# Four image layers in one kernel: first loads and evictions, the constants' products, a statistics product, layer 1's sums and the last evictions moved

## The chip, the cores and the metric

The kernel runs on one core of a Trainium2 chip. A core has five engines with a queue of instructions each: TensorE (PE) for matmuls and transposes, VectorE (DVE), ScalarE (ACT), GpSimd (POOL) and SyncE (SP), which here issues DMAs. PE writes to PSUM, which DVE and ACT empty into SBUF ("eviction"). An engine works through its queue in order, so an instruction that waits holds up what stands behind it. The metric is device time in microseconds (us), lower is better.

## The reference

The input `x` is float32 of shape (4, 64, 64, 64): four images of 4096 tokens with C = 64 channels. Four attention layers follow each other, each over the whole image:

```python
# layer 0: softmax(q k^T), read the other way round, gamma * out + x
attn = softmax(einsum('bic,bjc->bij', q, k)); out = einsum('bmn,bmc->bnc', attn, v); x = gamma * out + x
# layer 1: weights w / sigma_w (power step on w, u); phi and g max-pooled 2x2: 1024 keys
attn = softmax(theta @ phi.T); x = x + sigma * ((attn @ g) @ w_o + b_o)
# layer 2: group norm with 32 groups (per image row), attention per channel plane, residual
x = x + linear(attention(q, k, v of group_norm(x)))
# layer 3: group norm with 8 groups, attention scaled by 1/8, residual on the normalised h
h = group_norm(x); x = h + (softmax(q k^T / 8) v) wp + bp
```

## The kernel before

Tokens are kept transposed, two half images of 64 channels side by side on 128 partitions (`x_tile`, 128 x 2048). Wq and Wk of layers 0 and 3 are multiplied into one matrix beforehand ("form", `load_form` and `quadratic_form`); in layer 3 Wv and Wp likewise (`constants`).

A layer-0, layer-2 or layer-3 stage of one image is 64 *steps*. A step (`step`) issues two score tiles (`first`: four matmuls of 64 x 512 each, into an `s` tile), each followed by an exponential on ACT into a `p` tile, and then the sums of two earlier `p` tiles (`adds` or `then`) into accumulators. The 12 stages follow each other; their sums run a few steps behind their scores.

PSUM has eight banks: two `s` tiles of two banks each (pool `ps_s`), and four banks for accumulators (`ps_a`, `acc_tile`). Every score, projection, transposition and small product asks for the next `s` tile, and has to wait until the last tile in that buffer is read.

All other work is *background*: generators cut into pieces by `yield`. `background(tempo, ...)` sets how many pieces a step may take on average, and `advance` puts them at four places of a step: MID between its two groups of sums, LATE within the second, END after it. A piece marked ALONE goes to a MID and keeps LATE pieces (layer 1's scores) out of that step. `drain` runs what is left at a stage's end. So the order of the program is written by hand through these generators, and a `yield` more or less shifts all pieces behind it.

The places that matter here:

- *Opening.* ScalarE's queue loads Wq, Wk, bq of layer 0 and two of the eight first-half pieces of image 0 (L688 to L690, L651); SP loads the rest of the image (64 KB each) and then all other constants. PE transposes Wq and Wk (L715), multiplies them (L720, L721), transposes half the image (L892, in `transposed`), projects it to `q` (L859), transposes the other half, projects `q_swapped`, and only then starts layer 0's first step (L947). With `on="both"` the two halves of an eviction go to DVE and ACT, but from the same `s` tile.
- *Constants* (`constants`, L1523 on): small products with a MID between them: L1529, L1536 and L1538, L715, L720 and L721, L1551, L1556 and L1557, and for each of the four spectral norms L1582 and L1589.
- *Layer 1* (`layer1`): for image 0 with `bank=False`, sums added up on DVE; for images 1 to 3 with `bank=True`, sums in an accumulator (L1081). The denominators are L1097 on the running sums `zaccs` that DVE adds up (L1070), in an ALONE step, into an `s` tile.
- *Layer 3's statistics* (`before3`): DVE reduces the two halves (L1370), adds the two (L1372), and PE multiplies by the averaging matrix (L1374) in the same piece.
- *End.* The last block of queries: ACT copies one accumulator (L1210), DVE adds the other (L1211), PE multiplies by `wv3` (L1226) and sums the denominators (L1229, `lanes`), DVE takes the reciprocal (L1232), multiplies (L1234), adds `hb` (L1426), four DMAs write it (L1429). Then `rest_in_range` checks the softmax sums of this block (L1658 to L1665) and writes the flag `bad`. All engines load it (L1683) and branch over the second, general path (L1684).

## Time and profile before

| what | us |
|---|---|
| median of three timed runs | 3014.73 (3014.7 to 3015.45) |
| profiled execution | 3015.44 |
| its span, first to last instruction | 3013.7 |
| PE busy | 2979.1 (99%) |
| ACT busy | 1943.1 (64%) |
| DVE busy | 1769.4 (59%) |
| mean granted PE clock | 0.998 |
| from the span's start to the first score matmul (L947) | 15.4 |
| from the last sums to the span's end | 11.5 |

An engine's busy share says which engine bounds the whole, not which bounds a stretch. The chain of waits follows the last instruction back, at each step to what released it; in order of time its rows read "start, length, what". A row "PE s L947 x16" is one step's two score tiles (PE's records come in pairs, two for one float32 matmul). A row of waits reads "engine line <- who it waited for: total us, how often, the longest".

### The profile page before, as it was taken

The numbers are of one execution on the slowest core, as the hardware profiler recorded it, in microseconds if no ns is written. First come the engines' busy times: TensorE is split into PE (matmuls) and PEld (weight loads), VectorE is DVE, ScalarE is ACT, GpSimd is POOL, SyncE is SP. The second block draws the span as 40 slices with busy tenths as digits, with TensorE's granted clock in tenths as the row PEclk, the third lists the DMA queues.
The fourth block names the chain that finished last, engine by engine and source line by source line (L and its number), as shares of the span: only waits on it lengthen the run. The fifth ranks groups of instructions, "written<-read, shape, count | busy, mean of one in ns | idle before, by whom it ended". The sixth has DMA issues, their size and how long they took to land.

```text
span 3013.7 us, 64736 instructions
## 1 busy us (share of the span) xinstructions
PE 2979.1 (99%) x28501; PEld 1129.7 (37%) x28501; DVE 1769.4 (59%) x2058; ACT 1943.1 (64%) x2815; POOL 33.7 (1%) x35
## 2 busy tenths in 40 slices
PE   8999999999999999999999999999999999999998
PEld 3333233433444433344443333333343334333333
DVE  1221333588731068772017887777887777877777
ACT  6877777665578866557885655555555655555554
POOL 0000000000000000000000000000000000000000
PEclk9999999999999999999999999999999999999999
DMA  2010000000001000000000000000000000000000
GB/s 37 1 29 5 1 1 1 19 1 1 15 1 29 1 5 2 15 1 12 4 2 5 1 1 15 19 5 8 5 19 8 15 2 1 19 5 5 9 5 9
DMA packets 42081, 25.79 MB, mean 9 GB/s; under 512 B 39872, under 2 KB 39872, under 8 KB 40384
## 3 DMA queue, kind: packets, MB, share of 16 engines
q1 hardware_dynamic: 40464, 21.28, 3.4%
q8 instruction: 225, 3.69, 0.5%
q14 instruction: 64, 0.52, 0.1%
q10 hardware_dynamic: 1328, 0.30, 0.0%
HBM read 4.79 MB, written 4.19 MB: 3 GB/s over the span
## 4 chain that ended last, share of the span: by engine, by line
PE 97%; ACT 1%; DVE 1%; issue 0%; DMA 0%; ACTq 0%; DVEq 0%
PE acc L1203 29%; PE s L1168 29%; PE acc L972 15%; PE s L947 15%; PE s L1055 2%; PE acc L1081 1%; PE s L859 1%; ACT p L1061 1%; PE s L1081 1%; PE s L1226 1%; DVE zacc L1179 1%; PE s L878 1%; PE s L1312 0%; PE s L892 0%; PE s L1224 0%
## 5 line engine op out<-in xcount | busy, mean ns | idle before, releaser
L1173 ACT ACTIVATE p<-s 128x1024 f32<-128x1024 f32 x1024 | 994.7, 1022 | 710.8 <-PE s L1168 699.1
L1179 DVE TENSOR_TENSOR zacc<-zacc,p 128x1024 f32<-128x1024 f32 x960 | 1173.5, 1222 | 372.8 <-ACT p L1173 333.5
L951 ACT ACTIVATE p<-s 128x1024 f32<-128x1024 f32 x512 | 519.8, 1015 | 42.7 <-PE s L947 23.7
L1203 PE MATMUL acc<-p,v 64*64 64x512 f32 (+1 forms) x4456 | 526.5, 558 | 0.0
L972 PE MATMUL acc<-p,vs 64*64 64x512 f32 (+1 forms) x4224 | 514.0, 578 | 0.5 <-ACT vs L961 0.5
L1168 PE MATMUL s<-q,k 64*64 64x512 f32 x2048 | 495.0, 593 | 2.1 <-ACT p L1061 2.1
L1203 PE MATMUL acc<-p,hT 64*64 64x512 f32 x4096 | 494.1, 590 | 0.0
L947 PE MATMUL s<-xT,q 64*64 64x512 f32 x2048 | 488.3, 592 | 2.8 <-DVE v L879 0.6
L947 PE MATMUL s<-xT,q_swapped 64*64 64x512 f32 x2048 | 489.2, 592 | 0.0
L1168 PE MATMUL s<-q,xT 64*64 64x512 f32 x2048 | 486.8, 589 | 0.0
L1168 PE MATMUL s<-q,h_swapped 64*64 64x512 f32 x2048 | 479.3, 589 | 0.0
L1168 PE MATMUL s<-q,k_swapped 64*64 64x512 f32 x2048 | 476.9, 593 | 0.0
L953 DVE TENSOR_REDUCE all_z<-z 128x1 f32<-128x4 f32 x128 | 20.1, 157 | 622.3 <-ACT p L951 622.3
L1203 PEld LDWEIGHTS acc<-p,v 64*64 64x64 f32 x4456 | 179.8, 133 | 285.7 <-issue 280.6
L972 PEld LDWEIGHTS acc<-p,vs 64*64 64x64 f32 x4224 | 174.7, 133 | 266.4 <-issue 202.8
L961 ACT ACTIVATE vs<-v,all_r 64x64 f32<-64x64 f32 x512 | 176.6, 345 | 147.1 <-PE acc L972 72.3
L1203 PEld LDWEIGHTS acc<-p,hT 64*64 64x64 f32 x4096 | 156.3, 133 | 264.2 <-issue 263.4
L947 PEld LDWEIGHTS s<-xT,q_swapped 64*64 64x64 f32 x2048 | 146.3, 133 | 146.3 <-issue 111.4
L947 PEld LDWEIGHTS s<-xT,q 64*64 64x64 f32 x2048 | 146.4, 133 | 135.6 <-issue 109.1
L1168 PEld LDWEIGHTS s<-q,h_swapped 64*64 64x64 f32 x2048 | 143.9, 133 | 141.2 <-issue 136.2
L1168 PEld LDWEIGHTS s<-q,k 64*64 64x64 f32 x2048 | 140.5, 132 | 148.2 <-issue 99.3
L1168 PEld LDWEIGHTS s<-q,xT 64*64 64x64 f32 x2048 | 143.3, 133 | 140.2 <-issue 138.2
(205 smaller groups left out, 1564.8 us busy)
## 6 DMA issues: line engine op xcount, KB each, us to landing
k_swapped<-k SPq DMA_DIRECT2D x8, 512.0 KB, 6.1
h_swapped<-xT SPq DMA_DIRECT2D x8, 512.0 KB, 5.3
out_dram<-turned SPq DMA_DIRECT2D x62, 64.0 KB, 1.8
xin<-in_x_dram SPq DMA_DIRECT2D x24, 128.0 KB, 4.2
q_swapped<-q SPq DMA_DIRECT2D x6, 512.0 KB, 5.4
pg<-pg SPq DMA_DIRECT2D x8, 128.0 KB, 2.3
xin<-in_x_dram SPq DMA_DIRECT2D x14, 64.0 KB, 2.2
xin<-in_x_dram ACTq DMA_DIRECT2D x2, 64.0 KB, 2.8
```

What stands on the lines that cost most here:

```text
L859: nc.tensor.matmul(s[half(e), chunk(i)], w[half(i), half(e)], rhs[half(i), chunk(2 * j + (1 - e if exchanged else e))], start=True, stop=True,
L878: nc.tensor.matmul(s[:, ds(k * P, P)], rhs[:, ds((g * 8 + k) * P, P)], w, start=True, stop=True)
L947: nc.tensor.matmul(s[half(e), chunk(i)], queries(m, i, e), k[half(i), chunk(c)], start=True, stop=True)
L951: nc.scalar.activation(p, s, AF.Exp, accum_out=zs[m][:, c : c + 1])
L961: nc.scalar.activation(vs[half(e), :], v[half(e), m, :], AF.Copy, scale=rz[half(e), m : m + 1])
L972: nc.tensor.matmul(acc[c][half(i), cols], vs[half(e), :], ps[2 * t + n][half(e), chunk(i)][:, cols], start=(m == 0 and e == 0), stop=(m == ...
L1055: nc.tensor.matmul(ss[e][half(m), chunk(i)], pgs[0 if e == d else 1][r, ds(n * P + m * C, C)], th[r, chunk(2 * j + i)], start=True, stop=True,
L1081: nc.tensor.matmul(acc[quarter(q), :], g[:, k, :], ps[j, k][q // 2][:, chunk(q % 2)], start=(k == 0 or not bank), stop=(k == NK - 1 or not ...
L1168: nc.tensor.matmul(s[half(e), chunk(i)], k[(j + i) % 2][half(i), ds(j // 2 * P + e * C, C)], q[half(i), chunk(c)], start=True, stop=True,)
L1173: nc.scalar.activation(p, s, AF.Exp)
L1179: add = lambda: nc.vector.tensor_tensor(zaccs[c], p0, p, ALU.add)
L1203: nc.tensor.matmul(accs[c][e][half(i), cols], v[half(e), j, :], p[half(e), chunk(i)][:, cols], start=(j == 0), stop=(j == NB - 1),)
```

## The change

- *Opening.* Two loading queues for Wq and Wk; the four first-half pieces with r < 2 on SP, the others on ScalarE's queue; the bias and the second half behind them on SP. Matmuls on zeros (`keep_busy`) run between the form's operations. The first transposes and projections write two accumulator banks (`banks`, while `now[0] < 2`), one evicted by DVE, one by ACT. Both first projections come before the second half's transposes, which become the first background piece (`rest`).
- *Constants.* The transposition of Wv joins those of layer 2's weights, the form's products and the Wv-Wp product join the row sums' products in one `s` tile, and the four spectral norms run side by side: one piece with four L1582 products, one with four L1589 products, their columns handled 4 wide.
- *Statistics' product.* One `yield MID` between DVE's sum and PE's product in `before3`.
- *Layer 1's sums.* With `bank`, the denominators go to an accumulator bank, without the ALONE step in front.
- *End.* For the last image's last block `final` takes the place of `turn` and `last`: the denominators first, copies and sums in two halves of 256 columns, the range check on POOL (`rest_in_range`), and `bad` computed (`count_bad`) before the second half's multiply-add; DMAs alternate between SP and ScalarE's queue as before.

```diff
-    load = [nc.scalar.dma_start]
+    load = [nc.scalar.dma_start, nc.sync.dma_start]
...
+    def load_bias(n, bq):
+        load[0](form[n][1], bq.rearrange("(c o) -> c o", o=1))
...
         load[0](w[0:C, 0, :], wq)
-        load[0](w[0:C, 1, :], wk)
-        load[0](b, bq.rearrange("(c o) -> c o", o=1))
+        load[-1](w[0:C, 1, :], wk)
...
-    load_form(0, 0, a["L0_conv_Wq"], a["L0_conv_Wk"], a["L0_conv_bq"])
-    load[0] = nc.sync.dma_start
-    on_scalar = lambda r, i: nc.scalar.dma_start if i and r >= 2 else nc.sync.dma_start
-    load_x(state[0], [(slice(0, 8), on_scalar), (slice(8, 16), lambda r, i: nc.sync.dma_start)])
+    idle = scratch[:, 12 * P : 16 * P]
+    nc.vector.memset(idle, 0.0)
+
+    def keep_busy(n):
+
+        for _ in range(n):
+            nc.tensor.matmul(s_tile()[:, 0:256], idle[:, 0:P], idle[:, 0:256], start=True, stop=True)
+
+    load_form(0, 0, a["L0_conv_Wq"], a["L0_conv_Wk"])
+    load[:] = [nc.sync.dma_start]
+    load_x(state[0], [(slice(0, 8), lambda r, i: (nc.sync if r < 2 else nc.scalar).dma_start)])
+    load_bias(0, a["L0_conv_bq"])
+    load_x(state[0], [(slice(8, 16), lambda r, i: nc.sync.dma_start)])
...
+    def banks(on):
+
+        if on == "both" and now[0] < 2:
+            bank = [acc_tile(), acc_tile()]
+            return bank, bank
+        s = s_tile()
+        bank = [s[:, chunk(i)] for i in range(2)]
+        return bank if on == "both" else s, bank
+
...
-            evacuate("DVE", dst[:, 0:m], src[:, 0:m], bias)
-            evacuate("ACT", dst[:, m:], src[:, m:], bias)
+            evacuate("DVE", dst[:, 0:m], src[0], bias)
+            evacuate("ACT", dst[:, m:], src[1], bias)
...
-            z = s_tile()[:, 0:512]
+            z = acc_tile() if bank else s_tile()[:, 0:512]
...
         def finish(j):
-            yield ALONE
+
+            if not bank:
+                yield ALONE
...
         nc.vector.tensor_tensor(sums, stat[:, 0:1], stat[:, 1:2], ALU.add)
+        yield MID
         t = s_tile()[:, 0:1]
         nc.tensor.matmul(t, avg3, sums, start=True, stop=True)
...
+        def final(acc, sums):
+
+            z = acc_tile()[:, 0:8]
+            add_quarters(z, sums)
+            z_columns, r_columns = check_columns(8)
+            nc.vector.tensor_copy(z_columns, z)
+            nc.vector.reciprocal(r_columns, z_columns)
+            rest_in_range(z_columns, r_columns)
...
+            for m in range(2):
+                o, cols = o_tile("o")[:, 0:256], slice(m * 256, m * 256 + 256)
+                nc.scalar.copy(o, acc[0][:, cols])
+                nc.vector.tensor_tensor(o, o, acc[1][:, cols], ALU.add)
+                s = s_tile()[:, 0:256]
+                for n in range(2):
+                    nc.tensor.matmul(s[:, ds(n * P, P)], o[:, ds(n * P, P)], wv3, start=True, stop=True)
+                turned.append(s)
+            set_bad = count_bad()
+            for m, s in enumerate(turned):
...
+                if m == 0:
+                    set_bad()
...
-    st0 = transposed("both", s0)
-    next(st0)
-    alone(quadratic_form(0, 1.0))
-    next(st0)
-    queries0 = first_queries(s0)
-    next(queries0)
-    next(queries0)
-    alone(st0)
-    alone(queries0)
+    keep_busy(2)
+    form_transposes(0, s_tile())
+    keep_busy(1)
+    t = s_tile()[:, 0:P]
+    form_product(0, t)
+    form_scaled(0, 0, t, 1.0)
+    st0 = transposed("both", s0)
+    next(st0)
+    next(st0)
+    t = s_tile()[:, 0:1]
+    form_bias(0, t)
+    form_scaled(0, 1, t, 1.0)
+    keep_busy(1)
+    alone(first_queries(s0))
...
+        nc.tensor.transpose(s[0:C, 384:512], wvp[:, 0, :], ident)
...
+        yield MID
+        form_transposes(3, s_tile())
         yield MID
         t = s_tile()
...
+        form_product(3, t[:, 128:256])
+        form_bias(3, t[:, 513:514])
+        nc.tensor.matmul(t[:, 256:320], wvT, wvp[0:C, 1, :], start=True, stop=True)
+        nc.tensor.matmul(t[:, 320:384], bvb, wvp[0:C, 1, :], start=True, stop=True)
...
+        pt = s_tile()
+        for i, (r, d) in enumerate(shapes):
+            nc.tensor.matmul(pt[:, i : i + 1], ones[:r, :], sq[:r, i : i + 1], start=True, stop=True)
+        yield from inverse_norm(rn, pt[:, 0:4])
...
+        pt = s_tile()
+        for i, (n, dsts) in enumerate(spectra):
+            (r, d), (w, u, s, vb) = shapes[i], loaded[n]
+            nc.tensor.matmul(pt[:, ds(i * P, d)], vb[:r, :], w[:r, :], start=True, stop=True)
+        for i, (n, dsts) in enumerate(spectra):
+            d, (w, u, s, vb) = shapes[i][1], loaded[n]
+            nc.vector.tensor_copy(s, pt[:, ds(i * P, d)])
+            nc.vector.tensor_tensor(u, s, s, ALU.mult)
+            nc.vector.tensor_reduce(col(sq, i), u, AX.X, ALU.add)
...
-    background(1.0, second_half(s0), pause(6), constants(), loads(s1), pause(6), before0("DVE", s1), loads(s2))
+    background(1.0, rest(st0), second_half(s0, s0["v"]), pause(6), constants(), loads(s1), pause(6), before0("DVE", s1), loads(s2))
...
-    def rest_in_range():
+    def rest_in_range(z, r):
         assert checks[0] == NCHECK
...
+        nc.gpsimd.tensor_scalar(in_range[:, 0:count], z, SUM_MAX, None, ALU.is_le)
+        nc.gpsimd.tensor_scalar(in_range_r, r, 1.0 / SUM_MIN, None, ALU.is_le)
+        nc.gpsimd.tensor_tensor(in_range[:, 0:count], in_range[:, 0:count], in_range_r, ALU.mult)
+
+    def count_bad():
         nc.vector.tensor_reduce(least, in_range, AX.X, ALU.min)
-        t = s_tile()
+        t = acc_tile()
         nc.tensor.matmul(t[0:1, 0:1], least, ones[:, 0:1], start=True, stop=True)
-        nc.vector.tensor_scalar(bad, t[0:1, 0:1], -1.0, float(P), ALU.mult, ALU.add)
-
-    s3["after"] = rest_in_range
+        return lambda: nc.vector.tensor_scalar(bad, t[0:1, 0:1], -1.0, float(P), ALU.mult, ALU.add)
```

## The prediction

> **What bounds the kernel now.** The page first: who is busy, and who carries the chain that ended last.

> ```profile
> PE 2979.1 (99%) x28501; PEld 1129.7 (37%) x28501; DVE 1769.4 (59%) x2058; ACT 1943.1 (64%) x2815; POOL 33.7 (1%) x35
> ...
> PE 97%; ACT 1%; DVE 1%; issue 0%; DMA 0%; ACTq 0%; DVEq 0%
> ```

> TensorE (PE) is the bound almost everywhere, so an edit is worth only what it takes out of PE's own queue, or out of the two ends where PE does not yet, or no longer, run at full rate. The chain of waits was read next, in order of time, for the opening and for quiet and disturbed steps of the middle.

> ```profile
> 1.40 2.35 DMA scratch<-in_L_conv_Wk_dram
> 3.76 2.69 DMA xin<-in_x_dram
> 6.75 1.96 PE s L892 x8
> 8.73 0.70 DVE xT L838
> 9.48 2.60 PE s L859 x8
> 12.08 1.91 PE s L892 x8
> 15.38 2.57 PE s L947 x16
> ```

> The opening is serial, and PE is slow in it: eight transposes of L892 take 1.94 to 1.97 us here, and the same eight later take 1.02:

> ```profile
> 190.98 1.02 PE s L892 x8
> ...
> 104.82 0.86 PE acc L972 x8
> 105.68 0.31 PE s L1582 x2
> 105.99 1.02 PE acc L972 x8
> 107.01 1.72 PE s L947 x16
> ```

> The last four lines are the price of a small background piece: a plain step is 1.72 (scores) + 1.72 (sums); the piece adds its own 0.31 and 0.16 to the sums behind it (1.02 for 0.86), together 0.47. Next, who made PE wait, the layer-1 piece, and the one place where the clock fell:

> ```profile
> PE s L1374 <- DVE sums L1372: 4.1, 4, 1.2
> ...
> 656.44 0.99 PE s L1097 x8
> 657.43 1.02 PE acc L1203 x8
> ...
> 307.80:311.20 3.40, 3.40 (x20) 0.77 (x16) 2.08 (x2) 1.78 (x4) 0.00 (x0) 0.50 0.00 0
> ```

> The last of these (busy by engine, then granted clock, DMA share and GB/s) shows PE at half clock for 3.4 us in layer 1 of image 0. Last the end, from the instructions in order of time and from the line of the final branch:

> ```profile
> 3002.22 0.59 ACT L1210 COPY o<-acc 128x512 f32<-128x512 f32 x1 [4.03 <-PE acc L1203]
> 3006.15 0.69 DVE L1426 TENSOR_TENSOR turned<-turned,hb 128x512 f32<-128x512 f32 x1
> 3007.69 0.15 DVE L1665 TENSOR_SCALAR bad<-s 1x1 int32<-1x1 f32 x1 [0.37 <-PE s L1664]
> ...
> L1684 PEldq COMPARE_BRANCH  x1: 4035/4035/4035, 3008.6 to 3008.6; - x1
> L1684 ACTq EVENT_SEMAPHORE  x1: 17/17/17, 3011.8 to 3011.8; - x1
> ```

> The flag `bad` is the last thing computed; every engine then loads it (0.62 to 0.86), and PE's branch over the other path takes 4.04, while the output is long landing. ACT needs about 3.2 from its branch (3008.6) to its next event, DVE about as long. The span ends at 3013.7, some 0.9 after PE is through.

> **The change, part by part.** The working is against the profiled execution: 3015.44 us, of it 3013.7 span. The median of the three timed runs is 3014.73, so 0.7 is taken off at the end.

> 1. *Opening.* Before, the first exponential starts at 17.14. After: Wq and the four first-half loads of rows r>=2 are issued by ScalarE's queue, Wk and the other four by SP's; the bias load and the second half go behind them. ACT's issues cost 0.56 to 0.61, so its last one starts at 0.81+0.56+3x0.61 = 3.2 and lands 2.2 to 2.8 later (the issue table's medians): 5.4 to 6.0, where the chain had 6.45. Say PE begins the transposes at 5.9 (before 6.75). Each half then lies in two banks: DVE (0.69) and ACT (0.59) evict side by side instead of one after the other, and the second half's transposes leave the opening for the first main step. If PE is at full clock by then: transposes 1.02 with eviction behind until 7.6; both projections from 7.65 take 2x0.86 plus about 0.2 latency, to 9.6; DVE evicts the second by 10.35; scores of 1.07 (the L947 row); first exponential at 11.5. At half clock the transposes cost 1 more (12.5); if the projections are slow too, about 1.5 more (14.0). I take 11.7. What is late next: the second half's transposes, now in step 1, whose ACT eviction queues behind two exponentials (2 x 1.02), and values pushed one step on. Followed through the `s` buffers (each freed by one exponential or one 1.22 DVE eviction), the times from the first exponential are: step 2's scores 2.3, values 4.5, step 3 6.4, values 8.8, step 4 10.7, its second scores 12.1 (after DVE's `v`), step 5 14.8, step 6 19.5, and the first undisturbed step 23.0; before it is 40.34-17.14 = 23.2. So the gain is 17.14-11.7+0.2 = 5.6; bounds 3.1 and 6.5. SP carries one bias load more between the halves (0.6), covered, since the second half is wanted only at about 12.5 and the SP rows put its last issue near 8.5.
>    The four added matmuls on zeros cost nothing up to the input's landing; the last can delay the projections by half a microsecond, inside these bounds. [...]
> 2. *Constants.* The order of the changed program has 5 small PE pieces where there were 14. Before, the excess over a plain step of the 14 steps sums to 7.3: eight spectral pieces at 0.47 to 0.52, and six others at 0.40 to 0.75 (start to start of the steps). After: five transposes 0.79, the two form transposes 0.48, all products 1.7, the four L1582 products 0.31+3x0.24+0.16 = 1.2, the four L1589 1.3. But DVE now reads one `s` tile many times (seven reads of the products, 0.15 to 0.35 each, about 1.9; the fourth spectral copy as tenth instruction at 0.2, about 2.0), while the next-but-one scores want that buffer 0.86+0.16+0.86 = 1.9 later, and one batch also waits 0.4 for the row sums: stalls of 0.5 and 0.2. Gain 7.3-6.2 = 1.1; bounds -0.5 (both stalls 1 us longer) and 2.2 (none, and pipelined loads).
> 3. *Statistics' product.* DVE's sum of 0.15 then has a whole step to finish; PE's 4.1 of waiting goes. Behind it in PE's queue were sums and scores of the step, which is why all of it counts. The product still costs 0.47, as L1392's does (0.31 + 0.16). What follows slides by one or two steps in stages that have dozens to spare. Gain 4.1, bounds 3.5 and 4.2.
> 4. *Layer 1's sums.* For images 1 to 3, z takes a bank of the accumulators and needs no step of its own. Image 0's form is unchanged. Two L1097 pieces per image cost 0.99+0.16 = 1.15 each, some 1.2 by start to start. After, the first sits directly behind the L1081 sums, the second behind L1116. They keep 0.86 to 0.99, so each saves 0.2 to 0.3; six make 1.4, less a little for ACT's extra copy in a step of exponentials: 1.2. The new wait is z's on DVE's running sums, in front of scores: in the trace the last such add of image 1 ends at 639.13 (two L1070 rows from 636.78) and the sums before z at about 639.4, so it is just hidden. Bounds -1.5 (one 0.45 stall each) and 2.
> 5. *End.* z's product and reciprocal move ahead of the copies, the copy is halved, the range check goes to POOL, and `bad` comes between the last two multiply-adds. From 3002.2: z on DVE to 3003.24; two half adds (0.16+0.27 each, from the 512 and 1024 rows) to 3004.2; POOL's three small operations of 0.1 to 0.55 (its memsets and L748) to between 3003.7 and 3004.9; the rest of DVE to 3006.5 (3007.0 if POOL is slow), against 3006.84. `bad` is done near 3005.6, so PE's 0.65+4.04 run under the evictions, to 3010.4. Then ACT's queue is the last: two issues 0.9, load 0.62, branch to event 3.26: 3011.4, and 0.9 more gives 3012.3. Gain 1.4, bounds 0.3 (slow POOL, branches no faster) and 2.0; I take 1.3.
>    [...]

> Sum: 5.6+1.1+4.1+1.2+1.3 = 13.3. 3015.44-13.3 = 3002.1, and against the median 3001.4; I say 3001.5.

> **Rivals.**
> *Cold opening.* PE stays at half clock through the projections and the added matmuls only stand in the way. For it: the clock record starts at 14.2 and the matmuls before are slow though PE was busy from 9.5. Against: the zeros keep PE busy from about 1.5. Part 1 gives 3.1: 3004.
> *Better than summed.* The merged pieces hide, and the dip at 307.8 (its two rows 1.75 and 2.83 against 1.06 and 1.97 two steps on, 1.5 us) does not come back since the stage starts 7 us earlier. All upper bounds would be 3015.44-17-1.5; a plausible share is 17 in all: 2997.7.
> *The covers are gone.* z waits for DVE in all six places (1.2, one add, each) and both merged batches stall 1 us longer: 13.3-7.2-1.6 = 4.5: 3010, within 0.2%.
> *Slower.* The dip recurs. Layer 1 of image 0 has some 15 steps of 6.68 in which PE stops for an exponential (1.03); only one falls to half clock in this trace. The stage starts at another time, and if the fall came in every step it would cost 15 x 1.5 = 22: 3023. From nine falls on, it eats the 13.3. Against: the other fourteen steps do not trigger it.
> *It does not do what it says.* The program's order shows all the moves, so only the clock remains open, which is the first rival.

> **How the numbers follow.** Forecast 0.63, cold opening 0.16, better 0.12, covers gone 0.07, slower 0.02. The forecast's own range, from parts 2, 4 and 5 half-way to their bounds, is 2998.5 to 3005. The range to hold 8 in 10 reaches into the cold opening with weak parts 2 and 4, and into the better case: 2996.5 to 3007. About 0.2%, 6 us, is what a measurement of this kernel tells from nothing, so 3008.7 is the border: faster 0.91, same 0.06, slower 0.03.

> **What would show it.** Part 1: first exponential near 11.7, second-half transposes after it in about 1.02, a plain step by 35. Part 2: five pieces, the last before 100 us, with 0.2 to 0.6 of waiting on DVE behind the products and the second batch. Part 3: no wait of L1374's line on the sums. Part 4: z's wait on DVE under 0.2. Part 5: `bad` before the last two DVE operations, PE's branch ended before ACT's, under 10.5 us from the last sums to the end. Wrong it would be by a slow clock at the first projections, or several falls near 300 us.

## The result, and the profile after

The changed kernel takes 3005.69 us (median of 8 runs, 3004.41 to 3006.02) where the kernel before takes 3014.75 (8 runs beside it, 3013.88 to 3015.49). The ratio is 0.9969, with a 95% interval of 0.9958 to 0.9980. The time lies in the range that was given, and the direction is right, but the sum was too large: 13.3 us were forecast, and between the two profiled executions (3015.44 and 3005.78) there are 9.7.

The page of the changed kernel, busy time by engine and then the chain that ended last by engine:

```profile
PE 2979.2 (99%) x28509; PEld 1133.0 (38%) x28509; DVE 1760.1 (59%) x2003; ACT 1943.8 (65%) x2816; POOL 34.1 (1%) x32
...
PE 98%; ACT 1%; SPq 0%; DVE 0%; issue 0%; DMA 0%; ACTq 0%; DVEq 0%
```

PE's busy time is the same 2979 us, but it is not the same work: the matmuls on zeros add 4.5 us at the start (2.07, 1.22 and 1.22), and about as much went elsewhere. DVE's 1% of the chain is gone. Where the time went is read by setting the start of the same exponential in both traces side by side (there are 1664, and the program has them in the same order):

| stage, up to the exponential number | before | after | gain so far | gain of the stage |
|---|---|---|---|---|
| opening, 13 | 41.27 | 40.02 | 1.24 | 1.24 |
| constants and image 1's preparation, 107 | 218.30 | 215.62 | 2.69 | 1.45 |
| first pieces of layer 1 of image 0, 161 | 317.95 | 313.89 | 4.05 | 1.36 |
| layer 1 of images 1 to 3, 971 | 1745.54 | 1741.26 | 4.28 | 0.23 |
| the four statistics, 1481 | 2676.67 | 2668.20 | 8.47 | 4.19 |
| the end, span | 3013.71 | 3003.70 | 10.01 | 1.54 |

Differences are formed before rounding. 0.35 of the 10.01 is lost outside the span, which makes 9.66. The table says at once where the forecast was off: the opening gave 1.2 instead of 5.6, layer 1's sums 0.2 instead of 1.2, and 1.4 came from a place that the sum did not count.

The opening of the changed kernel: PE's instructions in order of time (weight loads left out), then ACT's.

```profile
5.97 1.97 PE L916 MATMUL acc<-ident,xin 128*128 128x128 f32 x8 [0.18 <-DMA scratch<-in_L_conv_bq_dram]
...
7.87 0.58 PE L736 MATMUL s<-scratch 64*128 64x1 f32 x2
...
8.39 1.22 PE L703 MATMUL s<-scratch 128*128 128x256 f32 x2
...
9.54 3.47 PE L883 MATMUL acc<-xT,A 64*64 64x512 f32 x16
...
12.83 1.02 PE L971 MATMUL s<-xT,q 64*64 64x512 f32 x4
```

```profile
7.98 0.59 ACT L870 COPY xT<-acc 128x512 f32<-128x512 f32 x1 [2.90 <-PE acc L916]
11.64 0.69 ACT L872 ACTIVATE q<-acc,Ab 128x512 f32<-128x512 f32 x1 [3.08 <-PE acc L883]
13.11 0.69 ACT L872 ACTIVATE q_swapped<-acc,Ab 128x512 f32<-128x512 f32 x1 [0.78 <-PE acc L883]
14.98 1.02 ACT L975 ACTIVATE p<-s 128x1024 f32<-128x1024 f32 x1 [1.18 <-PE s L971]
```

The eight transposes (L916) take 1.97, as slowly as before. ACT has emptied its half at 8.57, but the projections (L883) start at 9.54: a matmul on zeros (L703) stands in front of them. And they take 3.47, not 1.9. By these times PE is at half clock until 12.65, where the trace's record of the granted clock begins: the transposes before it start 0.213 apart, the same transposes of the second half, at 15.72, 0.109 apart. So the first exponential is at 14.98.

The other parts, from the chain in order of time: the two batches of spectral products, and the statistics' product L1409 (L1374 before) beside its twin L1427 (L1392).

```profile
89.48 1.06 PE s L1668 x8
...
101.00 1.14 PE s L1678 x8
```

```profile
1764.91 0.31 PE s L1409 x2
...
1779.14 0.31 PE s L1427 x2
```

L1409 has disappeared from the list of PE's waits; its steps take 3.91 to 3.94, like L1427's. Layer 1's denominators (L1121, L1097 before), first and second of image 1, same view:

```profile
634.56 1.00 PE acc L1105 x8
635.55 0.86 PE acc L1121 x8
```

```profile
692.67 0.86 PE s L1140 x8
693.53 1.00 PE acc L1121 x8
694.53 1.02 PE acc L1234 x8
```

And the end, in order of time (DVE and ACT), then the line of the branch:

```profile
2993.75 0.65 ACT L1480 COPY o<-acc 128x256 f32<-128x256 f32 x2 [4.03 <-PE acc L1234]
...
2996.71 0.14 DVE L1761 TENSOR_SCALAR bad<-acc 1x1 int32<-1x1 f32 x1
2996.78 0.40 DVE L1490 TENSOR_TENSOR turned<-s,all_r 128x256 f32<-128x256 f32 x1
2997.21 0.43 DVE L1494 TENSOR_TENSOR turned<-turned,hb 128x256 f32<-128x256 f32 x1
```

```profile
L1779 PEldq COMPARE_BRANCH  x1: 4152/4152/4152, 2997.5 to 2997.5; - x1
...
L1779 PEldq EVENT_SEMAPHORE  x1: 51/51/51, 3001.7 to 3001.7; - x1
L1779 ACTq EVENT_SEMAPHORE  x1: 17/17/17, 3002.2 to 3002.2; - x1
```

`bad` is now written ahead of the last two operations of DVE. PE loads it under them, its branch of 4.15 starts at 2997.49, just before the last of them ends (2997.64), and is through before ACT's queue. From the last copy to the span's end there are 9.95 us instead of 11.49.

### The profile page after: what moved, and what is told of

Read it like the earlier page. It is cut to its first block, busy times and chain, and to the rows that moved or that the text cites. A ratio compares the mean times of both kernels' runs of the same rounds, so it can differ in the third digit from the quotient of the medians.

```text
span 3003.7 us, 64700 instructions
## 1 busy us (share of the span) xinstructions
PE 2979.2 (99%) x28509; PEld 1133.0 (38%) x28509; DVE 1760.1 (59%) x2003; ACT 1943.8 (65%) x2816; POOL 34.1 (1%) x32
## 3 DMA queue, kind: packets, MB, share of 16 engines
HBM read 4.79 MB, written 4.19 MB: 3 GB/s over the span
## 4 chain that ended last, share of the span: by engine, by line
PE 98%; ACT 1%; SPq 0%; DVE 0%; issue 0%; DMA 0%; ACTq 0%; DVEq 0%
PE acc L1234 30%; PE s L1199 30%; PE acc L996 15%; PE s L971 14%; PE s L1079 2%; PE acc L1105 1%; ACT p L1085 1%; PE s L883 1%; PE s L1105 1%; PE s L1262 1%; PE s L1346 0%; PE s L902 0%; PE s L1260 0%; PE s L1443 0%; PE s L1366 0%; PE s L1051 0%
## 5 line engine op out<-in xcount | busy, mean ns | idle before, releaser
L1210 DVE TENSOR_TENSOR zacc<-zacc,p 128x1024 f32<-128x1024 f32 x960 | 1174.1, 1223 | 372.2 <-ACT p L1204 334.4
```

What stands on the lines that cost most here:

```text
L1210: add = lambda: nc.vector.tensor_tensor(zaccs[c], p0, p, ALU.add)
```

## The experiments

Two theories were to be told apart for the opening, both of them assumptions of the author's. The first: the clock rises after a stretch of some 3.4 us that PE fills with work (the fall in the trace of before lasts 3.413, from 307.793 to 311.206), such stretches lie at another place in each execution, and the kernel's short pauses waste them. The second: the clock rises at a fixed time, and the matmuls on zeros only stand in the way. For the other parts the question was whether each gives what the table of stages says. Every kernel is the changed one with one edit, except its repetition and the last kernel, which has two. The line numbers of an experiment can be some lines off. Clock and first exponential are from its one profiled execution:

| kernel | median us (runs) | profiled | clock rises at | first exponential | clock falls in layer 1, image 0 |
|---|---|---|---|---|---|
| before | 3014.75 (8) | 3015.44 | 14.25 | 17.14 | 307.79 |
| changed | 3005.69 (8) | 3005.78 | 12.65 | 14.98 | no |
| changed, again | 3005.47 (7) | 3005.88 | 14.48 | 15.38 | no |
| opening of before | 3007.37 (10) | 3007.22 | 15.86 | 18.01 | no |
| no zeros | 3004.51 (6) | 3004.56 | 10.65 | 13.60 | no |
| no last zeros | 3004.43 (6) | 3004.97 | 11.68 | 14.04 | no |
| zeros fill the pauses | 3004.77 (6) | 3003.94 | 7.99 | 12.85 | no |
| short fillers | 3005.17 (6) | 3005.61 | 10.89 | 13.98 | 304.44 |
| 10 us of zeros | 3007.33 (9) | 3007.33 | 7.02 | 16.62 | no |
| constants of before | 3007.06 (9) | 3008.94 | 13.03 | 15.16 | 306.58 |
| statistics of before | 3009.72 (11) | 3010.01 | 12.94 | 15.21 | no |
| sums of before | 3005.88 (7) | 3005.97 | 14.31 | 15.38 | no |
| end of before | 3007.26 (10) | 3007.32 | 12.50 | 14.89 | no |
| sums ahead of scores | 3003.18 (5) | 3002.34 | 12.95 | 14.35 | no |

The kernel before, run beside each of the four groups of experiments that follow, had medians of 3013.89, 3014.80, 3014.41 and 3014.88 us; so medians of different groups can be compared to about 1 us. The traces compare more closely: from the first to the 13th exponential all twelve traces with the changed order of the first steps take 25.03 to 25.05 us, and the two with the order of before 24.12 and 24.13. So what differs between openings is the first exponential, and 0.9 that the changed order gives back.

**The opening of before**

```diff
-    load = [nc.scalar.dma_start, nc.sync.dma_start]
+    load = [nc.scalar.dma_start]
...
-        if on == "both" and now[0] < 2:
+        if False:
...
-    keep_busy(2)
-    form_transposes(0, s_tile())
-    keep_busy(1)
...
+    st0 = transposed("both", s0)
+    next(st0)
+    form_transposes(0, s_tile())
...
-    background(1.0, rest(st0), second_half(s0, s0["v"]), pause(6), ...
+    background(1.0, second_half(s0, s0["v"]), pause(6), ...
```

> The changed kernel with the opening of before: its load order, no zero matmuls, first evictions from one score tile, the second half's transposes ahead of the first step. Theory: the opening is worth only 1.2 us of the 9.1, because the first exponential moved 2.2 and the transposes moved into the steps give 0.9 of it back; expected first exponential at 17.1, first step without background work again 1.2 us later than in the changed kernel, median 3006.9 (3006.5 to 3007.4). Rival: the forecast's 5.6 holds and another part lost the time; then 3011.

Median 3007.37, 1.7 to 1.9 above the changed kernel, as the first theory had it; the span is 1.54 longer. But its first exponential is not at 17.14, as was expected: the same opening is 0.9 later here. 0.1 of that is there from the transposes on (6.88 for 6.75), the rest comes in matmuls that run at half clock for longer (the second projection takes 1.97 instead of 1.23), since the clock rose at 15.86 instead of 14.25. So the same opening had a clock that rose at different times, and one trace of it is worth no more than about 1 us. The changed opening scatters less: six traces have it (the changed kernel's two, and those of the kernels with constants, statistics, sums and end of before), the clock rises at 12.50 to 14.48, and the first exponential is at 14.89 to 15.38. This run undoes the opening as a whole; what its load order, its two banks and its moved transposes give each was not run.

**No zeros, and no last zeros**

```diff
-    keep_busy(2)
     form_transposes(0, s_tile())
-    keep_busy(1)
     t = s_tile()[:, 0:P]
...
-    keep_busy(1)
     alone(first_queries(s0))
```

> The changed kernel without any of its four matmuls on zeros. The product for the bias then ends near 8.4 and the projections can start when ACT has evicted, at 8.65 instead of 9.54. Theory (the clock rises after a stretch of about 3.4 us of PE work without a pause): PE's work before 8.65 has pauses, so the clock rises only near 12 to 15; projections 3.4 us at half clock, first exponential 14.0 to 15.0, total within 1 us of the changed kernel. Rival (the clock rises at a fixed time, 12.65, whatever PE does): first exponential at 13.6 to 13.9, total 1.0 us less, 3004.6.

The second kernel takes away the last `keep_busy(1)` alone:

> The changed kernel without the last of the zero matmuls, the one in front of the projections (8.39 to 9.54 in the trace). Theory: projections start at 8.65, but PE then pauses 0.2 in front of them; if such a pause costs a whole stretch, the clock rises at 14 or later and the first exponential is at 14.4 to 14.8; if it does not, it rises near 12.65 as before and the first exponential is at 13.8. Rival (the zero matmul costs nothing because the projections waited for something else): first exponential unchanged at 14.98. Total 3004.5 to 3005.7.

Without the last zeros, PE's instructions in order of time:

```profile
7.92 0.58 PE L736 MATMUL s<-scratch 64*128 64x1 f32 x2
...
8.43 3.65 PE L883 MATMUL acc<-xT,A 64*64 64x512 f32 x16
```

The projections start 1.1 earlier and the first exponential 0.94 earlier (14.04); the last kernel of the table has this opening too, and there it is at 14.35. So the rival that the zeros cost nothing is gone. Without any zeros the clock even rose at 10.65 and the first exponential was at 13.60. Both kernels are 1.0 to 1.3 faster by their medians, little more than what groups can be compared to, but in the direction that the traces show. Neither theory had forecast this: the first one had the clock rise between 12 and 15 without zeros, and 13.60 and 3004.51 are the numbers of the second (13.6 to 13.9, 3004.6). Its cause, a fixed time of 12.65, is excluded all the same, by the rises of these two and by the changed kernel's own repetition, where the clock rose at 14.48:

> The changed kernel once more, beside the others, for a second record of its clock. Theory (windows of 3.41 us that lie at another place in each execution; the first one that PE fills without a pause raises the clock): PE has no pause from 5.97, so the clock rises between 9.4 and 12.8, at another time than 12.65; the first exponential moves with it, between about 13.6 and 15.0. Rival (a fixed time): 12.65 and 14.98 again. Median 3005.0 to 3006.0.

The theory missed here too. It had a rise by 12.8, because PE is busy without a pause from 5.98. The clock rose only at 14.48. So a window that PE fills by the trace's busy time was not enough here.

**Filling the pauses**

```diff
-    def keep_busy(n):
+    def keep_busy(*widths):
 
-        for _ in range(n):
-            nc.tensor.matmul(s_tile()[:, 0:256], idle[:, 0:P], idle[:, 0:256], start=True, stop=True)
+        for n in widths:
+            nc.tensor.matmul(s_tile()[:, 0:n], idle[:, 0:P], idle[:, 0:n], start=True, stop=True)
...
-    keep_busy(2)
+    keep_busy(256, 256, 128)
...
-    keep_busy(1)
+    keep_busy(256, 64)
...
-    keep_busy(1)
+    keep_busy(64)
```

> The zero matmuls sized to fill PE's pauses at 3.2, 4.7 and 8.5 (widths 256, 256, 128 ahead of the form's transposes, 256 and 64 ahead of the product, 64 ahead of the projections; pauses left under 0.2). Theory: PE works without a pause from 1.5, the clock rises by 8.4 at the latest, the projections from 8.7 take 1.9, the first exponential starts at 11.8 to 12.2, 3 us earlier than in the changed kernel; total 3002.5 to 3003.5. Rival (fixed time of the clock, 12.65): first exponential at 13.7 to 14.0, total 3004.6.

The clock rose at 7.99 and the projections ran at full speed. PE in order of time:

```profile
6.48 1.81 PE L916 MATMUL acc<-ident,xin 128*128 128x128 f32 x8
...
8.89 2.01 PE L883 MATMUL acc<-xT,A 64*64 64x512 f32 x16
```

2.01 stand against 3.47. The first exponential came at 12.85, 2.1 earlier than in the changed kernel, not 3: the wider zeros pushed the form back (its transposes by 0.4, the input's by 0.5). The median of six runs is only 0.7 to 0.9 lower, which two groups do not tell apart, and nearer to the rival's 3004.6 than to the theory's 3002.5 to 3003.5. Three runs lie at 3003.48 to 3003.94, the traced one among them, and three at 3005.59 to 3006.47; when the clock rose in these is not known. The second try kept the fillers small:

```diff
-    keep_busy(2)
+    keep_busy(256, 256, 32)
     form_transposes(0, s_tile())
-    keep_busy(1)
+    keep_busy(256, 32)
...
     form_scaled(0, 0, t, 1.0)
+    keep_busy(64)
...
-    keep_busy(1)
     alone(first_queries(s0))
```

> The changed kernel with zero matmuls that bridge the short pauses (32 columns ahead of the form's transposes and ahead of the product, 64 behind the product until the input lands) and none ahead of the projections. Theory: PE is without a pause from 1.5, the clock rises between 4.9 and 8.4 wherever the windows lie, the projections start near 8.45 at the full clock; first exponential at 12.4, or down to 11.5 if it rises before the transposes. Total 2.6 us under the changed kernel's profiled 3005.78, 3003.2, where no fall of the clock in layer 1 of image 0 adds some 1.5. Rival (the 32-column fillers are too short to count): the clock rises between 9.4 and 12.9 as in the changed kernel, first exponential 13.5 to 14.2.

This theory failed: the clock rose at 10.89, as the rival said. PE in order of time:

```profile
4.13 1.49 PE L703 MATMUL s<-scratch 128*128 128x256 f32 x4
5.54 0.79 PE L732 MATMUL s<-scratch 64*128 64x128 f32 x2
6.27 0.69 PE L703 MATMUL s<-scratch 128*128 128x64 f32 x2
6.75 1.91 PE L916 MATMUL acc<-ident,xin 128*128 128x128 f32 x8
```

No row has idle time in front of it: by the trace PE is busy without a pause from 1.50, as the theory wanted, and the clock stayed low all the same. So it is not idle time in the profile that held the clock down here. The fillers also moved the product from 5.00 to 5.54 and the input's transposes from 5.97 to 6.75. The last test puts dense work ahead of everything:

```diff
-    keep_busy(2)
+    keep_busy(*[512] * 6)
...
-    keep_busy(1)
     t = s_tile()[:, 0:P]
...
-    keep_busy(1)
     alone(first_queries(s0))
```

> The changed kernel with six matmuls on zeros of 512 columns ahead of everything else and no others: PE is dense from 1.5 to about 11, and the form and the input wait behind them. Theory (the first window of 3.41 us that PE fills raises the clock, zeros or not): it rises between 4.9 and 8.4, and the matmuls on zeros are shorter behind that point; total 1 to 3 us more than the changed kernel. Rivals: zeros do not count, then it rises 3.4 to 6.8 us after the last of them, near 15 to 19; a fixed time, then near 12 to 15.

The line of the zeros in that kernel, durations as minimum, median and maximum in ns, and PE in order of time:

```profile
L703 PE MATMUL s<-scratch x12: 592/888/1222, 1.5 to 9.1; 128*128 128x512 f32 x12
```

```profile
1.50 8.14 PE L703 MATMUL s<-scratch 128*128 128x512 f32 x12 [1.50 <-DVE scratch L698]
...
10.99 1.06 PE L916 MATMUL acc<-ident,xin 128*128 128x128 f32 x8
```

The clock rose at 7.02, in the middle of the zeros, which then ran in 0.59 instead of 1.06, and the transposes behind took 1.06. So zeros counted as work, and 5.5 us of wide matmuls on them (1.50 to 7.02) were enough in this execution.

What has to fill a window is read here from the same traces, afterwards, and was not tested. Count only the columns that PE streams, at the speed that the transposes show at half clock (0.213 us per 128 of them, from start to start in the changed kernel). Then the windows after which the clock rose were filled to between 0.78 and 1.00, and those after which it did not to at most 0.81. In the changed kernel two windows were missed: one filled to 0.72 (six gaps of 0.13 to 0.23 between the columns, nearly all of it inside what the profile counts as busy) and one filled to 0.70 (the bias product L736 and the zeros around it). With the short fillers the missed window from 4.07 to 7.48 has 0.68. The border is near 0.8 in these traces; windows of 0.78, 0.79 and 0.81 did nothing, others of 0.78 and 0.81 were enough, so this count alone does not decide it. The transposes have to be counted: they are 1.46 of the 3.41 us in the window of 0.78 that was enough (4.58 to 7.99, where the zeros fill the pauses).

**One part undone at a time.** The statistics' product:

```diff
         nc.vector.tensor_tensor(sums, stat[:, 0:1], stat[:, 1:2], ALU.add)
-        yield MID
         t = s_tile()[:, 0:1]
```

> The changed kernel without the new piece boundary between DVE's sum and PE's product of the statistics. Theory: the four steps of the product return from 3.94 to 5.2, 4.8, 4.8 and 5.1, and PE's wait for the sums to 4.1; median 4.2 more than the changed kernel, 3009.9. Rival (the wait had gone because the whole schedule shifted): under 2 more.

PE's waits in it:

```profile
PE s L1408 <- DVE sums L1406: 4.1, 4, 1.2
```

Median 4.0 to 4.3 more. The constants one by one again (`constants` as it was, with a piece for each product; its first lines):

```diff
         for i in range(4):
             nc.tensor.transpose(wt[:, i, :], wl2[:, i, :, :].rearrange("p j f -> p (j f)"), ident[:C, :C])
-        nc.tensor.transpose(s[0:C, 384:512], wvp[:, 0, :], ident)
...
-        form_product(3, t[:, 128:256])
-        form_bias(3, t[:, 513:514])
...
+        form_transposes(3, s_tile())
+        yield MID
+        t = s_tile()
+        form_product(3, t[:, 0:P])
```

> The changed kernel with the constants' products of before, one by one. Theory: fourteen small pieces cost 7.3 over plain steps where the five merged ones cost 5.9; median 1.4 more than the changed kernel, 3007.1. Rival (the merged pieces' stalls on DVE eat the gain): within 0.3.

Median 1.4 to 1.6 more, and 1.44 between the exponentials 1 and 109 of the two traces. The five merged pieces have 5.9 us over plain steps, the fourteen small ones 7.3. The sums of layer 1:

```diff
-            z = acc_tile() if bank else s_tile()[:, 0:512]
+            z = s_tile()[:, 0:512]
...
-            if not bank:
-                yield ALONE
+            yield ALONE
```

> The changed kernel with layer 1's denominators as before: an own step in front and a score tile for all images. Theory: the bank saves only some 0.1 an image (0.3 where the product now stands directly behind sums of the same tile shape, nothing behind the output product, and 0.2 lost when DVE's work slides into the steps of the evictions); median within 0.5 of the changed kernel, 3005.5 to 3006.1. Rival (the forecast's 1.2 holds and is lost elsewhere): 3006.8.

Median 0.2 to 0.4 more, with a first exponential that was 0.40 later; between exponentials 287 and 971, that is layer 1 of all three images, the difference is 0.23. The chain of this kernel, at the place of the first denominators:

```profile
652.79 0.99 PE s L1121 x8
653.78 1.02 PE acc L1233 x8
```

0.99 and 0.16 behind it (1.02 for 0.86) is what the product costs alone. In the changed kernel the first one costs 0.86, with sums of the same tile shape in front of it (`128*32` both), and the second one 1.00 and again 0.16, behind a product of `64*64`. The end:

```diff
-            st, wv3, "p (i n) f -> p n i f", last, not_before, "done3", final if st["b"] == B - 1 else None
+            st, wv3, "p (i n) f -> p n i f", last, not_before, "done3"
...
+            if c == NC - 1 and "after" in st:
+                st["after"]()
...
+    s3["after"] = rest_in_range
```

> The changed kernel with the end of before: copies and sums in one piece, the range check behind the last eviction. Theory: from the last sums to the span's end 11.5 instead of 10.0, median 1.5 more, 3007.1. Rival (the engines' branches set the end wherever the flag is computed): under 0.5 more.

Median 1.6 to 1.8 more; from ACT's last copy to the span's end 11.41 instead of 9.95.

**The falls of the clock, and a faster kernel.** In three of the fourteen profiled executions the clock fell for one window in layer 1 of image 0. Busy time by engine, then granted clock, in the windows around the fall with the short fillers:

```profile
301.03:304.44 3.41, 2.88 (x36) 0.78 (x32) 0.93 (x3) 2.20 (x4) 0.00 (x0) 1.00 0.00 0
304.44:307.85 3.41, 3.41 (x24) 0.84 (x20) 1.75 (x2) 2.05 (x5) 0.00 (x0) 0.50 0.00 0
```

and the same in the changed kernel, where it did not fall:

```profile
302.76:306.18 3.42, 2.89 (x34) 0.66 (x34) 1.51 (x4) 2.13 (x3) 0.00 (x0) 1.00 0.00 0
306.18:309.59 3.41, 3.41 (x42) 1.21 (x38) 1.02 (x1) 3.22 (x7) 0.00 (x0) 1.00 0.00 0
```

Both windows hold PE's 0.53 of pure waiting for an exponential behind the second piece's scores (L1079, 1.6 us in that piece). What differs is where in the window the wait ends: at 2.82, 3.16 and 3.31 of 3.41 in the three falls, at 0.63 to 2.70 in the changed kernel and the nine other traces that have this wait. The place alone is not enough: ten other waits of 0.53 in this layer end between 2.82 and 3.31 of their window too (the first piece's in the changed kernel at 2.89), and no fall followed. The two steps that a fall touches take 15.07 to 15.33 instead of 13.89, so 1.2 to 1.4 us. Why the clock fell at this wait is open: by the count of columns the windows ahead of the falls are filled to 0.71 to 0.73, but so are many that no fall followed.

The wait itself is PE's longest (8.0 us in 15 steps), so the last run took it away, together with the last matmul on zeros:

```diff
+            order = [(m, e) for m in range(2) for e in range(2)]
+            for m, e in order if bank else sorted(order, key=lambda me: me[1]):
...
                 yield LATE
+                if n and not bank:
+                    add(*todo[n - 1])
                 accumulate = scores(*todo[n])
-            if n:
+            if n and (bank or n == len(todo)):
                 yield END
```

> The changed kernel without the last zero matmul, and with layer 1 of image 0 in another order: the sums of a piece go directly ahead of the next piece's scores (at LATE instead of END), and the scores of the two halves are issued one half after the other, so that the sums' tile is read by DVE while the first half runs. Theory: PE's wait for the exponentials (15 steps of 6.68, each with 0.53 of pure wait and more around it) goes, at the price of scores that take 1.71 instead of 1.28; steps of 6.2, 7 us less in all; and because the falls of the clock come behind that wait, none is recorded. Opening as without the last zero matmul. Median 2997.5 (2996 to 3000). Rival (the scores' half-array order costs what the wait did): steps of 6.6 to 6.9, median 3004 to 3007.

Its chain in order of time:

```profile
314.17 0.99 PE s L1105 x8
315.17 1.90 PE s L1079 x16
317.07 0.59 PE acc L996 x8
```

The wait is gone, and nothing stands in its place but the scores, which take 1.90 half by half (1.71 expected, 1.28 before). Thirteen of the fifteen steps take 6.39 to 6.56 and two 6.91, against 6.68: between the theory and its rival. Between the exponentials 107 and 421 the trace is 2.9 us shorter, where 7 were expected. The median is 3003.18 (5 runs, 3001.87 to 3003.70), 3.2 above the theory's range and 0.8 below the rival's; ratio to before 0.9961 (0.9947 to 0.9975). It is the lowest median here, but its interval overlaps that of the kernel without the last zeros (0.9954 to 0.9979), whose median is 1.25 higher in another group. No fall was recorded in its one trace, which shows little at three in fourteen.

## Why the prediction was right in its total and wrong in its opening

*Part 1, the opening: 5.6 forecast, 1.2 in the traces, 1.7 to 1.9 by the medians.* The step that failed is "If PE is at full clock by then", an assumption: by its terms the first exponential was at 11.5 (11.7 was taken), and it came at 14.98. Three terms make most of the 3.5. The transposes took 1.97 instead of 1.02, as they had before: 1.0. The projections took 3.5 instead of 1.9 to 2.0: 1.5. And the zeros that were to keep PE busy held the projections up for 0.9; "the last can delay the projections by half a microsecond" was too low. Input (5.97 for 5.9) and the way from the projections' end to the first exponential (2.0 for 1.9) were right. The rows had shown the slow transposes behind PE work (1.97 at 12.01 in before, directly behind the projections), and the rival "cold opening" went by them. The choice between it and the sum went the wrong way by the reason "the zeros keep PE busy from about 1.5": by the profile they did, but for one pause of 0.18, and PE was at half clock until 12.65 all the same. What the clock goes by instead is known only as far as the count of columns above goes. So this rival came true, and worse than the 14.0 that it had.
The second half of that step failed too: from the first exponential to the first undisturbed step 24.1 were measured and 23.0 forecast (23.2 before). The moved transposes of the second half (1.09 at 15.72) lie on the path there, and the scores behind them wait another 0.44 for DVE's eviction of them.

*Part 2, the constants: 1.1 forecast, 1.4 measured.* Five pieces, the last of them at 101. The stalls of 0.5 and 0.2 were too large: the step behind the products and the one behind the second batch take 3.59 instead of 3.43, so 0.16 each.

*Part 3, the statistics: 4.1 forecast, 4.1 to 4.2 measured,* by the stage and by the part undone. A wait that the list of waits prices, with nothing queued that takes its place, is worth what the list says. That held here; the row of 8.0 in layer 1 of image 0 gave only 2.9, because its removal made the scores longer.

*Part 4, layer 1's sums: 1.2 forecast, 0.2 measured.* The step was "each saves 0.2 to 0.3". That held for the first of each image (0.29), not for the second: 0.99 plus 0.16 was the price of this product (`128*32`) behind `64*64` products, with or without a step of its own. And some 0.2 an image went to DVE's operations, which slid into a step of the evictions: the step behind the row of L1260 takes 3.64 instead of 3.43 (at 717.07 in image 1), where DVE starts on the tile 0.6 behind the product instead of 0.2.

*Part 5, the end: 1.3 forecast, 1.5 measured.* POOL was fast (0.20 to 0.24 an operation), `bad` came before the last two operations, and ACT's queue ended last, as followed.

*What was not in the sum.* The dip at 307.8 was a rival's term ("better than summed") and was taken to hang on when the stage starts. In these traces it goes with where the windows lie in that execution. So 1.4 of the 9.7 us between the two profiled executions are luck; with the fall, by the same 1.4, the changed kernel's trace would be at about 3007.2 (an estimate). The "slower" rival, with many falls, did not occur; no trace has more than one. "The covers are gone" did not occur either: z's line is not in the list of PE's waits, whose smallest row is 0.2.

So 13.3 became 9.7: 4.4 less in the opening, 1.0 less in the sums, 1.4 more from the clock, 0.7 more in the other three parts and 0.35 less outside the span. The time held the range because the range reached into the cold opening, and because no fall of the clock came on top.

## What to carry to other kernels

Price a wait on the bounding engine by its row in the list of waits, and check what is queued behind it and what its removal makes longer; but price a moved matmul by its own duration next to its new neighbours, because here the change of tile shape was paid wherever it stood (1.00 for 0.86, and 0.16 behind it). In an opening, do not take PE's busy time for a PE at full clock: look where the clock rises, and at how much of each window of 3.4 us wide matmuls fill (here 0.78 or more ahead of each rise). A filler in front of ready work cost nearly its length (0.9 of 1.15 here). Compare two openings by several executions, since one trace was 0.5 to 0.9 us off by itself here.

## What the runs showed of the hardware that was not expected

The moment at which PE's clock rose spread over 1.6 to 2.0 us between executions of one and the same opening (14.25 and 15.86; 12.50 to 14.48 in six traces). Being busy in the profile did not raise it by itself: with the short fillers PE has no pause from 1.50, and the clock rose at 10.89. Matmuls on zeros alone did raise it (at 7.02, in the middle of 8.14 us of zeros), while products of a single column (L736, two records in 0.58) are busy time with almost no columns. The clock fell for exactly one window of 3.41 us although PE had waited no longer than 0.53 in one go, in three of fourteen traces, and always behind the same wait, though ten others of its length at the same places of a window had no such effect.
